# A four-layer recurrent kernel: the chunk inverse of layer 0 solved on 16x16 quarters, the last feed-forward's variances as columns, and a new written-out order

## The chip, the cores and the metric

The kernel runs on one core of a Trainium2 chip. The metric is device time in microseconds (us) of one execution; the times below are of three runs.

The core has five engines, each with an instruction queue of its own that it works off in order: PE (TensorE, matrix products; its weight loads are listed apart as PEld), DVE (VectorE), ACT (ScalarE), POOL (GpSimd) and SP (SyncE, which here only issues DMA transfers). They wait for one another by semaphores. Data lies in an on-chip memory of 128 partitions; PE writes into eight banks of 512 columns, from which DVE or ACT evicts the result. All data is 32-bit, and a matmul shows up in the profile as two instructions (two passes), a transpose as one.

## The reference, cut to what matters

Two sequences of 1024 tokens with 128 channels pass through four layers, each an attention and a feed-forward. Layer 0's attention is a delta rule in chunks of 32 tokens, 4 heads of 32:

```python
T = -einsum('bhnid,bhnjd->bhnij', k * beta, k)      # (k beta) k^T of a chunk, 32x32
T = where(tri_strict, T, 0.0)
for i in range(1, 32):                              # forward substitution
    T[..., i, :i] += einsum('bhnj,bhnji->bhni', T[..., i, :], T[..., :, :i])
T = T + eye(32)                                     # inverse of a unit lower triangle
u, w = T @ (v * beta), T @ (k * beta)
# then a scan over the 32 chunks: S = S + k_i^T (u_i - w_i S), o_i = q_i S + attn (u_i - w_i S)
```

The outputs of this rule, of two depthwise convolutions (7 and 25 taps) and of v itself are mixed by a small routed network. In layer 3 the feed-forward has two inner layers of local attention and a gated product behind a layer norm:

```python
mu, var = h.mean(-1), h.var(-1)
h = (h - mu) / sqrt(var + 1e-5) * lg + lb
a, g = split(h @ w1 + b1, 2)
x = x + (a * gelu(g)) @ w2 + b2
```

## The kernel before, in words

The kernel is first recorded and then issued. Every operation that `program` and the stage functions call goes to a recorder (`Record.note`), which bundles neighbouring small matmuls of one shape (up to 32) into one unit. Each unit knows which earlier units it depends on. A string, `ORDER`, is decoded into a list of all 7156 unit numbers, with a bit for each eviction that may run on DVE or ACT, which says which of the two takes it. `Record.issue` (its call is line 603, so that the profile names L603 for nearly every instruction) emits the units in that order. A second string, `PLACES`, says which physical buffer each tile gets. So each engine's queue is exactly the order's subsequence for that engine; no planner runs at build time. The two sequences (batches 0 and 1) are independent of one another, and the order interleaves them. The stage functions `l0_attn`, `l0_ffn`, `l1_attn` and so on are called per layer and per batch in `program`.

**Layer 0's attention** (`l0_attn`). After the projections and short convolutions, keys are transposed, normalized and kept in `ka`; `vk` holds, per token, v times beta and normalized k times beta (two DVE products per group out of the transposes' bank). Products of keys, 32x32 per chunk and head, land in the banks `kk`; DVE multiplies them by the mask `mb` (minus beta, strictly below the diagonal) into `nn`. Since the substitution works along rows, the 128 triangles (32 chunks x 4 heads) are brought one to a partition: eight transfers by way of the memory `scr_n` and one back into `ncol`. The substitution loop has 31 steps; step i multiplies i x i elements (`prod`) and sums them into column i of `u`. The result goes out to `scr_u` and returns in four transfers to `td`, tokens on partitions again. Then come `pu` (td times vk, 32x32 blocks at four row positions of the array, 64 matmul instructions a bank) and its eviction `uw`, then `chunk` and `au` products, the scan of 30 steps (`next` on PE, `state` on DVE), the outputs `o`, the convolutions on DVE (`conv`, 7 and 25 passes of 1024 columns), features, the small network (`rh`, `logit`), `mixed` and the output projection into `s`.

**Layer 3's feed-forward** (`l3_ffn`, `Block.forward`, eight times: two batches, two inner layers, two blocks of 512 tokens). Channels are on partitions. The product with the constant matrix `center` takes off the mean; ACT squares; the product with the constant `mean` (all 1/128) gives each token's variance in all 128 rows (`var`, 128x512); scale, root and reciprocal then run on 128x512, and `z` is multiplied by the result. `b2` is added by POOL after DVE has added the products `down`. `Block.forward` of the last block is followed by `close`, which gates and stores the output.

`t512` tiles have 512 columns and 21 buffers; `arr` tiles have 1024 columns out of 35 larger buffers; `small` tiles have up to 64 columns.

Of the kernel before, what the change touches and what calls it, by code (L numbers as in the profile page):

```python
# [21 lines left out]
ALU = mybir.AluOpType  # L22
X = mybir.AxisListType.X
# [165 lines left out]
def _constants():  # L189
# [12 lines left out]
        "ident32": (p % 32 == c[:, :32]) * one,  # L202
        "quad4": (p // 32 == c[:, :4]) * one,
# [52 lines left out]
def pack_inputs(inputs):  # L256
# [40 lines left out]
    "c-mE22VfM%*WWk0S90kgotn@U6j7x2-n&vokRnwO5J+;jdzS=|sv=zoC{22o9;rd3D_ufKLJ8?1$>r{L=X*1I@$Yv@Hd|(AUj4n_n|r?Wm%yTt"  # L297
    "sY21Fc7zfTd`khK>_P_+kM<M|<sMVm>#(Ad6JxR(+^PK!go{57stj4>hHB}it4-jh+WR+GzXvA=ysi7H`me;`>65j8IQ%>~I#awlz*T72?3s3?"
    "&6XLjMgJw^F7zt)gH@A76+-im-fGkjc8s#k2q~&L(Un{T2gE6Pl^@ok8M}K0LqMsYVVdk;dJjS(U%#UjI!*bZFX}u3$d1UaRUDcd`y@0_1m!u1"
    "pt-@n()eHI0Ni^A<%TOhTBAf8p4<q((K~Jd{P(kM=gTYn<Ro-HwRbh1bTm|PXI0A_@1Jg{PBXvY4_9xgUUkub-dZ{fb_~6F-BQ22>FUW)-vm`5"  # L300
    "rZPOJ427UQNrMsVCY*RWA?HfdqwdKs(_VSTA8)!#at*m8F6y}F6A@GpQ$qX0Pot?HIKe=T&e+Vi1`-QdhUE*{^e@nw1`_tD4ip5#^W=38w!1zz"
    "#z1nyyoE4v%|vVE1tZj$+2iWMgL+(?N3I5VoHVH+zdGCQ`iK0)|Luvc?0;GdlM60p4gra{JDxR>d=ZLAAIu2{zy00IjRk-90odD_5}_!l1G&37"
    "0Zs;3h^6L3r$9hlK5I+Ph@Yp6h9dY;$@PB$HB_*zoihIgtaPpLc@;4|cwU*gFt?USk|u@aYi^UJFp`>22Uc;GZkfJhW~Fn1(RHQ_u1BLD2RiK8"
    "_n}^t3NQvX!q^$j0=jJgNEuT&X*=cePXB(gQJk5ze4E$G(^rk{2*0oRue;_<4i31v!ZR(ZGQhK}mMy2XNQ0ul!LZ|I#x}@(e!qBvcVIfxUo254"
    "{bcNYk=>Y8cYJCGfHg4bsdNZn{JYZ|ynP0(F7A?>KK;F8jjZJ9emE-fHAHKmncz8IRCz(vy>W{dTn^jNpYHlJL?S<Y8ddsE2DnYV+D>nJt;#<G"
    "Z$sv@y)!FMiwp9(5aqkHU#+E~ty;pxR<O1D{;8R#<(#lrQRk=J#>uu1gQqc%mz8hGEF<e@Y|LD>ATGlY1<wmDwE#xPtMx#!qkA9KS#Wdbv~~j_"
    ">eX(5fv6n5TPY95!q*tfTSkKa8z29-;8y~elNM-l7Qly)F)x18Mr~buI>XPegaj5rWND4qokO+Xf}z>L@*$wzdkK(BE0Z-7Om4Fa=7IZr0tWCv"
    "Da`a5jG1{VsH-Ngn*KekoPy`<qe|g<TEHuRaelXkVhC}jd_rKpO-oFepSb?}8;SAr$4B~>5n@eFNW#DQkX0?i61r^W>?M!ZO=<FG_UD~$E!q6}"
    "qB-!(jflA;8bZjp@$1F;C4Mg|-)S&+YE^(4UsuamW|*A&VMaBWHMeZtxEfzUJ7`=>d*U|M*2K~*F-j`8h}zSbf1uWr*rMFp^l>An^I4b{Af-PH"
    "2`Oy+rbMfCB@7@6Ue?G7IM5Faxy2j5sH%PO^Rvn?X{$?w7!B$&J1z5Vd*oev>d#OzZhOhNpLTqqQiH(*`Mwrs>uV)Wvni;sq}suzvzK_(>LUj&"  # L310
    "JJPF$Y_yd5NiNZl3DN!;TEH|}^A9R2ClT3T3Mhb(Y_e;T=9Ef&;O7xrRrthUE(?22oghh)h{n|<greMc;nn}5mw5l(c_$j+lo?$c7ICMfQh_JH"
    "=_v}<0;na|Xz+Eq*28OXzl2}P&1JsjJ|#eWoE9Ia=3ij4l=x6LjedpU5g~Hyi&nwqgKH70nnX%9YN8?)f&5&(rGa=%nr8A4NhJga;0vk|-<=GT"
    "w$8tsmR>WwyZSY(FBU;GAAo)bdbw3%7Rx7eJ+Z39&rdaYRLMkCO%n}|>fi)Ui^rh3BN4yyAyhR`1Dyv8Aq&C^Je6JMS>GD7qE(ZoN`#2`4k14$"
    "%WE!Dl^B3{M2|^wH@OA@PU;~>_qwlsnBMsiR4SyF5`U-V%R>*%uG;BZ?W{7R5mcwYNA*E1e2N2|)I4Z!?X<8QKe8yfNVF7cVW7q*)w$^>k{hv="
    "syr|74=?I*7*x&F<HB1J1(e(-@R;19QDqikULbha<N+|cMcUx$`kv5Y+pMJKJ}oc3mBj9cZpf#)93q1jUKri;z{M`<FzsO9{UZGJo>&L=y_;9*"
    "`x!1UspR&D^kt-_MDi^)5O`MD|5WFD7I;g1FSj$E>3Fre)AG3BQE7+z&K)(*Z2Tgm(aS+^3Qr6<1U;%GLe;i0TdGG{J{sp*Z+f=*<%qK$ktH-8"
    "H=*6JkN*meJ@4ClRGWyPLP$=^UOngKj`d%XlW=^|v@c(taFQAsv}fn|&@5A8`8W3))T>%Ib`}j2bGrN;kY4Ma@zb=q6QqdC*7YI;zLhBITB%-U"
    ")r*5nAwR;DUD-oV=6<;rNFb2GDPLY{{wnm>mKS00=A_5JLa9lNd$#MND~1Inely0xrhYqfD!W(L+Og$C+v`xJTHK;;DStlvIy-EeM2Cvfp3=D6"
    "mvS@aLHdJUzn=Tf89>0^_}J>ZRp)d&tgihs97+&MELhjFEwf@pQfy(VMM}QdE*Vt~N&`ir($XMGd_<ZZ`PyjGeAHFjUOptXvkTVFh31#r<=m+U"
    "5w75kQRGeS{H%b$x7vwL2EQ(UuI~~<8oNwaKey+-zkcQ4SzGS@f^>vrRh2X);!DTqO~D0m!}r?kO5%5CZ{PI!t|;lro>fmvEKcc%>Ao{JjUMwZ"  # L320
    "nYpCQmS|Y;&c&4FLs-2ZlX9iQCs*$cztLpFXMs+Y_$qUJsasq<#$b9hpx=SCZ@~>Cs=xRNY`!46MG51uv{EsqYN^RdAgBm})dC-Lxw%~3^-UI~"
    "H5SfOT|jap&UGs!m+ICk6^$CK-FHA60Q>U~jDfz#x^JjLwdJ!h`9-(HBGf=sqMFep6eHEF8p}R*>$p(jM@fxm{PfbA?*btW)0m|lkVDYNRn{Ni"
    "^tV&}_w^v6L3|aelF_hPk~F$`?VshEIdA{i4dd(IS999I{nC%`1Qb-NdMy|{H8Vg}Yd@}a3xdjh0Qw(-H^BwrZ|*=7f2UD1Q(9&=AcR?pCC%T7"
    "08)+?aiXUPm0T9JEVPW2OMZ+4M*NIQV~P0j4`>RLS5-h-jHO)C4nPm_LH*J$BPaU5j)b(B8~t6SJ_~24XX{sfvHH+8DKDz#-?y69PNzhqNGd!>"
    "`ltWhn>^hq-@o;`sO#l%OMm$FOv<;FM|!kHMejZ98dwxuGy5Bpl2>=#f<NQipYD{=qDJK6*!OP_{`JD@3)MH)9s108AxgbGtXi$j)ok_J2OmDT"
    "{#DiefpxxF{7ur}l~c}s7u%PW%_5`#)|mF!q3fIMQs4Ub*F~!TRBwK{-jdc$JM?TB4brB#<wL%L@1tzdLknLW{W5>Y%yo6PE-NiCjQH(fPJpTF"
    "-23|?Hg!I>JZ^YF-r<0AiK|Dcucda0k18jA(cxD3?D$`1hW0tsq&_$bjFX>zHg0#p)s1Vmto-P!ix*oolx4q?Rb6~v&R*K;%Gr&bV%LxD(-%fH"
    "yC!%x7tGqQdgj^<^?tei24H2kVLw&b1s%KXm^9J7a|HFf(sb3e51v5G?MBx|{_0oavR58Y7u!~x*ewJXEG}E%dG}t+M&J7a%*)<YsaEw3{q{Gm"
    "aU=H6rXT-S5d2RO(p3sKu5}{$zmJ05P0sg8D}<)^>qB;6I`qjt7X4B{A`nhSl>X-QmAbxq9aZJ6>G$_Cu{svC-y7Ho_Vn2{=g6&30cvlQN(`!L"
    ")TYl|y9a;WqCBif?R4bUsudHq8>Xi8%Sc6%5s)6#(@0VVRL!hPOk~ZnM_Re>^OzO=4)|T$XHZ6N$z5?zEc<yXY#Ir%Gsl_<Eev`}mWEXCXWH3+"  # L330
    "|A)R%<DW~=IIv1VSv2Ikj<?-8E;uYFhd`Z2MV|BH5mNqc2t`4+8kt`O7wnz&B=*V5v4>$~nL8xtJM?Yy@D<gEO6vA;*6LFyCW1L-*!H12#+0f4"
    "?t5hs-!E_mmlAjIRK?Hfmk|QnnuMNqe?}z3`gU*LId^<%o-df3xsO9gB;3D0al@}e-}}=zXnW&Z9SguWJg6`aQm4LvK_^}uZx5+o6yR#sHRU3G"
    "llWp`Ro|B3Z|hjYr>%P9>sK_#4oJg#og44tgpg}D20qyn3waQKx|7n+e@C-UN}JF_eT%Qxd(iks{*28eE%`z7+t(q_(ktKO_iO7Wxn;Y^guH^t"
    "ACq4%^Z0iQh)w%2J@U}wm}jx1gC(UP?pc)os?XL37u5D-mxj?^N8fyPqV2w3dz;-)Z(+FKXWJ*o#%)iJB6-LJ@3!d|ym%ml<!p)>v#4a|5)kC2"
    "fy3u4*-%!Ov^A0w2KZ+poF34wb9o!6SEaDuXEo{!pPaKRetyeZ8B$PgGx0is_j2wBzD0a9w!LH+GHpdb%7ykLm*1>CVRqF<w?2GUquuqaH$J|l"
    "FRo4?7yho9J|3~~Tvq2QS8A6=yUr0~;FFpk!|AX~K@Zz}yt-w9TMM#Hf}EXw!7%0Iqp9m%0XDyZ5!(vC2hw`GpVV`yN37Gc+3nQ4E8m{EH&L@R"
    "D*onk!%w5J!+B>#|BZcCObXc9y^+=Dais^fCpCElAsPOwFRfql_0H7Lxmx4-@%K&NUE6H88n!)reDP+-;nO~7a^n;8@}UQvH#e4>S0oJa`=Bf<"
    "I&a?hpX_l4_dGgQ)WnQ~C#%BTBcI=@vOts|@==}g%c*&bMjZJvWeiM>dH$r=6ptA?{VuwfjSCp{tJVs>i(O}RLZ0YnYX7@f;v){)>^Ep*C=~jX"
    "6h)gpFMV{=HNdnZKlGFG+b@epUU`<@G3Z{u%Uf3NfyiIlL-$m*_b%vlss`k0?T@xjJGcbn<fId{&?3L`QHM#Bs|!Z_G;LX8`p`D#kF9J0^Y$#A"
    "J>bwv-`aBr)9Du%!kM%ge|$H?_1!Vi4u^yGbiOeB)$BGSrv3I^<14c-1xv1?w04W@4*Y(|f>j5OnJyJ|pVbMjo=Jqgw;GyP)&6r1EG}*Rr|H|H"  # L340
    "l=P_ELkgXXomAs%aIURzt^;YUw23B90?T4zQqK-C)lAjS?WuN*%D=Apy>D^-QFFpeo18uK#b3S1G4pBY5Jk7QFm|{ybcEx9aT7p7a#N#F-Bb5r"
    "-7~HTS6v87-P+$*^9lDn-dDN(@9m+@gNAMeTBP-CGQWl2tA23xy-Te?7NzE)2j!%Wr^-)m-bx&YO;Bd3-0j)rlN(Ze1H>$!YI!C#(C5`F4@6eV"
    "i+$m)iS;$BX3Nz95rx6zL7i)XMa^%MAphK8cu51R-VF#dzo1p}EP3fSy2sW!33uVi!#`HR2iUd5o;uoF8{%7fg?30WRi=-(kBfrGwKA$@m4n*$"
    "a&__ksHfTPC#?ah{W&+)T=u6cYY1$snl)U44P#HY+#!7$wTzB!HRhAuBT@$!!lvlgQBwQA#j4K|rnDZi^WMwM8m%9_ke-g!u0l~nd58V|bN$V`"
    "J6e8tzdiQUtu*z@zz6+~-EfNo5B1$UFS+)NeqYs#&f5K`>DAspu3q##oZHh3&J8cis*<&P27RT`D;+{ikB44-GjLhcjLI*DoqF@4@+Z5py5D)P"
    "HX-L<*S}LG<ki)fPdw)hEiONQ*Qd?{NfVzz2e;9a;Sw`DYR}wR)uiZ`o;v^3)U>l5mNe0>_gYj?X=8f&7W<6Fvz8}rJRP%Z-l@)mp}Y&+dA+^="
    "uxYJCi$}Y-sWVj5o(^oZv8>gfljFBOx~KI$d342;9*6U74QJ-heO~?PJL1(Q*Ud#|`$TqIDejrG{B%pxK=7Q*O6&wbPV2mN$oY@1or2kZ-^@>I"
    "|J$mQ2al8fXLFUSXXBhHUnI`lF?n11+gakG^j5i~&j-6AvK~(iJN9w#nqepYil}`xpry<C%>1DDAHFqB;>F-G8%%WP`<2Lhm%2X8Ibp8bX5D~+"
    "Pm8WlQZLk}`ut(nD=+zo^rhGK8<8Oy>UUpWf8b7^K5($_zMCHgz8M;{@kZmJz8eDC*I6^@U>B#96O;1M)4nNfZ)@Gl4Eub#8l8KG?CNtm@Y7}f"
    "6P5>&{LfFcK2Ahqv8DT|4rS&e{f@Ru?QTeU4?a4dKj3#uwm-Bz($xSbTp=w}ONRamJ)+hd%(O)){Pv;6QWCjgcz)Wz{oPbkQ0`IMtMK^eMURHT"  # L350
    "wjqz-TDE^tUh@7ui{=Bl<`_e|Gb1v5P0NmPGn~faIvFX7DoF{8#fR^TTe^m;rB45CpOyzrO}5IGfD5GV^D58k2i$518xPv*`e$c?5-)aZ`E%`z"
    "YR5k)k8$N;-*g$eQc25x`+m84lr)OTtWoyF)cshEGKu<#=DVHAiOBMgj#o3*mX20$7-xT6>q)Jnz5f>91@l|Ot;Pn=!<wa`(vd-h+dnaCf3?wG"
    "`~A^8Hxw*oK#ul2k9|?c3&Ya?X!XO4-x@qJQcrPMv$PebI`4p2LeuA=eoeoR3V!@<8-N{fXjDmVEh*)*vs!Dd#5XgvQt?}Zs}i!+Dp}{-5$w#%"
# [454 lines left out]
def cols(t, n=1, w=P):  # L808
    return slice(t * w, (t + n) * w)


def l0_attn(C, w, xpad, b, out):

    nc = C.nc
    H, DH, CH = 4, 32, 32
    NTH = TB * H

    fold = xpad.shape[1] > L
# [1515 lines left out]
```

## Time and profile before

| | |
|---|---|
| median of the three runs | 1892.36 us (1890.59 to 1892.56) |
| the profiled execution | 1896.98 us |
| its span, first to last instruction | 1895.1 us |
| PE busy | 1749.1 us (92%), 14012 instructions |
| DVE busy | 1399.5 us (74%), 2855 instructions |
| ACT busy | 1065.3 us (56%), 1980 instructions |
| POOL busy | 423.2 us (22%), 436 instructions |
| mean granted clock of PE | 0.948 of full |

Busy times are of the whole span, over stages that differ in what bounds them; that is why the prediction goes by stretches. PE's instructions are pipelined and their ends modelled, so that a busy PE need not be at its peak. A group's line has the line, engine, operation, tiles (written<-read), shape and count, then after the bar the busy time of the group in us, the mean of one in ns, and after the second bar the idle time of the engine just ahead of them with what ended most of it. A timeline's line has start and duration in us, and in brackets the idle time before and its releaser; "SPq" is the issue of a transfer. A stretch's line gives its two ends, its length, the busy time and count of each engine, PE's granted clock, the share of DMA time and GB/s.

### The profile page before, as it was taken

The page shows a single profiled execution, that of the slowest core. Times are in us where ns is not written, and L with a number is a line of the kernel's source. Part 1 is how long each engine was busy: PE and PEld are TensorE (multiplying, and loading weights), DVE is VectorE, ACT ScalarE, POOL GpSimd, SP SyncE. Part 2 cuts the span into 40 slices and gives each one's busy share as a digit, 9 for nine tenths or more (in the row PEclk, how much of TensorE's full clock was granted, in tenths as well). Part 3 has the DMA queues.
Part 4 walks back from the last instruction along what each step waited for, and adds up shares of the span by engine and source line. Part 5 has one row for each costly group of instructions (what it writes and reads, how often), then busy time and mean ns, then how long its engine had stood idle before and what let it go on. Part 6 is the DMA issues. An engine that isn't in the chain of part 4 may idle for free.

```text
span 1895.1 us, 35145 instructions
## 1 busy us (share of the span) xinstructions
PE 1749.1 (92%) x14012; PEld 995.0 (53%) x14012; DVE 1399.5 (74%) x2855; ACT 1065.3 (56%) x1980; POOL 423.2 (22%) x436
## 2 busy tenths in 40 slices
PE   7985996769999999999999999999999999999996
PEld 4454555554227632384665577544346776444483
DVE  7995999796115544345989897878889989877866
ACT  5231232226996588836646454765656777765552
POOL 0010102212221242303002640224307411620000
PEclk9995996679999999999999998999999999999998
DMA  3110101002223321332223022002002120001020
GB/s 111 30 23 9 23 23 35 13 1 59 85 79 103 111 62 39 92 103 72 67 61 100 26 89 68 1 2 58 12 14 64 39 60 29 1 2 38 10 85 21
DMA packets 67908, 90.91 MB, mean 48 GB/s; under 512 B 29185, under 2 KB 41473, under 8 KB 67617
## 3 DMA queue, kind: packets, MB, share of 16 engines
q1 hardware_dynamic: 58624, 59.34, 10.6%
q0 software_dynamic: 9120, 29.33, 5.4%
q8 instruction: 110, 1.80, 0.4%
q14 instruction: 54, 0.43, 0.1%
HBM read 80.65 MB, written 8.00 MB: 47 GB/s over the span
## 4 chain that ended last, share of the span: by engine, by line
PE 66%; DVE 24%; issue 4%; ACT 3%; DMA 2%; SPq 1%; POOL 0%; POOLq 0%; DVEq 0%; ACTq 0%
PE sim L603 16%; PE num L603 8%; PE av L603 7%; DVE u L603 4%; PE tr L603 4%; DVE conv L603 3%; PE wo L603 3%; PE down L603 2%; PE up L603 2%; DVE e L603 2%; DVE prod L603 2%; PE qk L603 2%; PE z L603 2%; PE ph L603 2%; DVE ss L603 1%
## 5 line engine op out<-in xcount | busy, mean ns | idle before, releaser
L603 ACT ACTIVATE e<-sim 128x512 f32<-128x512 f32 (+3 forms) x896 | 429.5, 558 | 166.3 <-PE sim L603 78.2
L603 PE MATMUL num<-e,v 128*64 128x512 f32 (+4 forms) x1280 | 188.5, 427 | 1.9 <-ACT e L603 1.2
L603 DVE TENSOR_TENSOR e<-e 128x512 f32<-128x512 f32 (+3 forms) x320 | 177.1, 588 | 9.5 <-PE num L603 4.0
L603 PE MATMUL sim<-q,kT 64*128 64x512 f32 (+3 forms) x768 | 158.5, 513 | 7.1 <-ACT e L603 4.5
L603 PE MATMUL sim<-q,k 32*128 32x512 f32 x1024 | 149.2, 641 | 0.0
L603 POOL TENSOR_TENSOR sq<-qk,tab 128x256 f32<-128x256 f32 x128 | 105.6, 851 | 140.6 <-ACT qk L603 62.7
L603 PE MATMUL av<-e,va 128*32 128x512 f32 x1024 | 135.4, 606 | 0.0
L603 PEld LDWEIGHTS num<-e,v 128*64 128x64 f32 x1280 | 80.7, 137 | 91.1 <-issue 69.4
L603 ACT ACT_TABLE_LOAD x89 | 114.2, 1283 | 16.2 <-DVE g L603 6.1
L603 PEld LDWEIGHTS sim<-q,kT 64*128 64x128 f32 x768 | 73.4, 186 | 94.8 <-ACT e L603 45.1
L603 PE MATMUL ph<-h,w_f 128*128 128x512 f32 x256 | 114.7, 601 | 0.8 <-ACT h L603 0.8
L603 DVE TENSOR_TENSOR sim<-sim,const 128x128 f32<-128x128 f32 x256 | 65.3, 291 | 42.4 <-PE sim L603 39.5
L603 PEld LDWEIGHTS sim<-q,k 32*128 32x128 f32 x1024 | 44.4, 184 | 99.3 <-ACT e L603 74.1
L603 POOL TENSOR_TENSOR u<-u,sq 128x512 f32<-128x512 f32 x64 | 88.2, 1393 | 5.4 <-issue 3.1
L603 ACT ACTIVATE e<-e 128x320 f32<-128x320 f32 (+3 forms) x160 | 77.7, 529 | 19.7 <-DVE e L603 18.8
L603 DVE SCALAR_TENSOR_TENSOR conv<-vT,w_a,conv 128x1024 f32<-128x1024 f32 x60 | 84.0, 1409 | 0.8
L603 PEld LDWEIGHTS ph<-h,w_f 128*128 128x128 f32 x256 | 48.1, 192 | 57.5 <-issue 55.2
L603 POOL DMA_INDIRECT we<-in_experts,index x46 | 44.7, 973 | 148.5 <-issue 29.4
L603 POOL DMA_INDIRECT xg<-xd,index x46 | 44.5, 967 | 148.5 <-DVE index L603 65.3
L603 DVE TENSOR_REDUCE ss<-sq 128x8 f32<-128x512 f32 x96 | 62.8, 672 | 8.2 <-ACT sq L603 8.2
L603 PE MATMUL qk<-w_f,shifted 128*128 128x512 f32 x128 | 62.5, 608 | 4.9 <-DVE shifted L603 2.2
L603 DVE SCALAR_TENSOR_TENSOR e<-sim,const 128x320 f32<-128x320 f32 (+2 forms) x128 | 62.3, 528 | 5.9 <-PE sim L603 4.3
(521 smaller groups left out, 3568.9 us busy)
## 6 DMA issues: line engine op xcount, KB each, us to landing
zb<-zd SPq DMA_DIRECT2D x192, 128.0 KB
tab<-in_rotary SPq DMA_DIRECT2D x8, 512.0 KB
yd<-y SPq DMA_DIRECT2D x10, 256.0 KB
w_f<-in_f SPq DMA_DIRECT2D x4, 512.0 KB
mk<-in_mask SPq DMA_DIRECT2D x4, 512.0 KB
w_l<-in_l SPq DMA_DIRECT2D x4, 512.0 KB
w_f<-in_f SPq DMA_DIRECT2D x4, 448.0 KB
w_f<-in_f SPq DMA_DIRECT2D x2, 516.0 KB
```

Of the source, the lines that this page charges most:

```text
L603: tc.keep_in_program_order(f(*map(real, args), **{k: real(v) for k, v in kw.items()}))
```

## The change

Three things are edited, and the order and buffer strings are replaced.

In layer 0 the two 16x16 triangles on the diagonal of each 32x32 triangle are inverted side by side: the loop has 15 steps, and step i works on 2 x i x i elements. The part left of the second triangle (16x16) is no longer solved; it is kept as `ko`, unscaled products of keys under the new mask `off32`. `td` holds both inverses on its diagonal, zeros elsewhere, and is multiplied by beta once; so `vk` holds v and k without beta. With D for `td` the chunk's solution is D (x - ko D x): one round of `pu` matmuls, an eviction, a second round with `ko`, a subtraction on DVE and a third round and eviction.

In the last feed-forward the variances are taken with the squares as weights, so that each group of 128 tokens gives one column (128x4 in all); scale, root and reciprocal run on these four columns; four products of the column, spread over 128 columns, with the identity matrix bring the result back to 128x512 in a bank. The eviction of the centred bank to `z` may go to ACT or DVE by the order's bit, where it was DVE's. The addition of `b2` on POOL stands ahead of the gated products.

The new order has 7176 units. In it batch 0's layer-0 attention ends at place 781 (before: 975), batch 1's at 1225 (before: 1148).

```diff
+        "off32": ((p % 32 < 16) & (c[:, :32] >= 16)) * one,
...
-    nc.vector.tensor_mul(rbeta, beta, rk)
...
-        nc.vector.tensor_tensor(vk[g][:, :, 1], heads(ps), bview(rbeta, 4 * g, 4), ALU.mult)
+        nc.scalar.copy(vk[g].rearrange("p (t h) s d -> p t h s d", h=H)[:, :, :, 1], ka[g][:, :, 0])
...
-        nc.vector.tensor_tensor(vk[g][:, :, 0], heads(ps), bview(beta, 4 * g, 4), ALU.mult)
+        C.evac(vk[g][:, :, 0], heads(ps))
...
                 nc.vector.tensor_tensor(
+                    four(ko, g, hp)[:, hh], pv[:, :, 0, :], C.c["off32"].unsqueeze(1).to_broadcast([P, 4, CH]), ALU.mult
+                )
...
         for q in range(4):
+            for a in range(2):
+                nc.sync.dma_start(
+                    out=scr_n[q, cols(g, 1, 16), a].rearrange("n i j -> i n j"),
+                    in_=nn[cols(2 * q + a, 1, HC), cols(g, 1, 16), cols(a, 1, HC)],
+                )
...
+    for i in range(1, HC):
+        pv = prod[:, : 2 * i * i].rearrange("p (a m j) -> p a m j", a=2, m=i)
+        nc.vector.tensor_tensor(
+            pv, u[:, :, 0:i, 0:i], n4[:, :, i, 0:i].unsqueeze(2).to_broadcast([P, 2, i, i]), ALU.mult
+        )
+        nc.vector.tensor_reduce(u[:, :, 0:i, i], pv, X, ALU.add)
+    nc.sync.dma_start(out=scr_u.rearrange("q n a j i -> (q n) (a j i)"), in_=ul)
+    ta = C.arr("td")
+    nc.gpsimd.memset(ta, 0.0)
...
+                out=td[cols(2 * q + a, 1, HC), :, cols(a, 1, HC)], in_=scr_u[q, :, a].rearrange("n j i -> j n i")
...
-    for i in range(1, CH):
-        pv = prod[:, : i * i].rearrange("p (m j) -> p m j", m=i)
-        nc.vector.tensor_tensor(pv, u[:, 0:i, 0:i], ncol[:, i, 0:i].unsqueeze(1).to_broadcast([P, i, i]), ALU.mult)
-        nc.vector.tensor_reduce(u[:, 0:i, i], pv, X, ALU.add)
...
+    nc.vector.tensor_tensor(td, td, bview(beta, 0, TB), ALU.mult)
...
-            C.evac(uw[g][:, 8 * k : 8 * k + 8], pu.rearrange("p (n s d) -> p n s d", s=2, d=32))
+            x, y = (v[g][:, 8 * k : 8 * k + 8] for v in (vk, uw))
+            C.evac(y, times(td, vk, g, k))
+            nc.vector.tensor_tensor(x, x, times(ko, uw, g, k), ALU.subtract)
+            C.evac(y, times(td, vk, g, k))
...
-            nc.vector.tensor_copy(z, pc)
-            pn = C.bank("var")
-            C.mm(pn, C.c["mean"], sq)
-            C.rstd(r, pn, 1.0, 1e-5)
-            nc.vector.tensor_mul(z, z, r)
+            pn, pr = C.bank("vcol"), C.bank("roots")
+            for k in range(4):
+                C.mm(pn[:, k : k + 1], sq[:, cols(k)], C.c["mean"][:, :1])
+            C.rstd(r, pn[:, :4], 1.0, 1e-5)
+            for k in range(4):
+                C.mm(pr[:, cols(k)], r[:, k : k + 1].to_broadcast([P, P]), C.ident)
+            C.evac(z, pc)
+            nc.vector.tensor_mul(z, z, pr)
             nc.vector.tensor_scalar(z, z, w["lg"], w["lb"], ALU.mult, ALU.add)
+            nc.gpsimd.tensor_tensor(tiles(xb), tiles(xb), w["b2"].unsqueeze(1).to_broadcast([P, 4, P]), ALU.add)
...
             nc.vector.tensor_add(xb, xb, ps)
-            nc.gpsimd.tensor_tensor(tiles(xb), tiles(xb), w["b2"].unsqueeze(1).to_broadcast([P, 4, P]), ALU.add)
```

`times` holds the matmul loop of `pu` as it stood before, with the matrix as an argument.

## The prediction on record

> **What bounds the kernel now.** I read the page's 40 slices first, then the busy time by stretch, then groups inside the first 420 us, then two timelines.
>
> ```profile
> PE   7985996769999999999999999999999999999996
> DVE  7995999796115544345989897878889989877866
> PEclk9995996679999999999999998999999999999998
> ```
>
> A slice is 47.4 us. In the first nine VectorE (DVE) is fullest, TensorE (PE) has holes and its granted clock dips to 0.6; after that PE is at nine tenths almost throughout. The stretches say it in us:
>
> ```profile
> core 0: us, PE busy (x) PEld busy (x) DVE busy (x) ACT busy (x) POOL busy (x), PEclk, DMA share, GB/s
> 0.00:420.00 420.00, 333.92 (x4530) 208.16 (x4530) 358.37 (x639) 128.28 (x191) 55.24 (x52) 0.83 0.11 30
> ...
> 420.00:1000.00 580.00, 572.46 (x3913) 290.33 (x3914) 292.01 (x790) 398.67 (x728) 130.53 (x142) 0.98 0.26 76
> 1000.00:1840.00 840.00, 806.21 (x5345) 470.51 (x5345) 713.94 (x1382) 522.80 (x1041) 234.47 (x240) 0.99 0.13 39
> ```
>
> Layer 0 of both batches ends at 415 us (last write of `s`, batch 1: 415.5). Up to 420 us DVE works 358 and idles 62, of which 10 at the start and some 25 in batch 0's recurrence (`next`/`state`, 144 to 182 us). So layer 0 is DVE's. From 420 us to 1840 us PE idles 42 us in 1420: DVE savings there can win only from those. The last 55 us are one chain.
>
> **Part 1, substitution (layer 0).**
>
> ```profile
> L603 DVE TENSOR_TENSOR prod<-u,ncol 128x1 f32<-128x1 f32 (+30 forms) x62 | 34.6, 558 | 1.7
> L603 DVE TENSOR_REDUCE u<-prod 128x1 f32<-128x1 f32 (+30 forms) x62 | 31.2, 504 | 1.9
> L603 PE MATMUL pu<-vk,td 32*32 32x64 f32 x512 | 11.8, 257 | 5.3 <-issue 4.6 <-DMA td<-scr_u 0.7
> ...
> L603 DVE TENSOR_TENSOR mixed<-mixed,rms 128x1024 f32<-128x1024 f32 x4 | 4.9, 1219 | 0.0
> ...
> L603 DVE TENSOR_TENSOR nn<-kk,mb 128x128 f32<-128x128 f32 x16 | 3.9, 281 | 0.7 <-PE kk L603 0.6
> ```
>
> Step i of the old loop works on i² elements, i = 1 to 31. The tile's rows give 0.140 us at one element and 1.16 at 961, so 0.139 us + 1.063 ns an element. The new loop has i = 1 to 15 on 2i²: 30 instructions of 0.139 (4.2 us) and 2 x 2480 elements (5.3 us), 9.4 us a batch. Old 34.6 + 31.2 = 65.8 us for both batches, new 18.9: **47 us less**. Added on DVE, both batches: 16 `ko` products at 0.281 (4.5), two scalings of `td` at 1.22 (2.4), eight subtractions of 512 columns at 0.68 (the DVE rows of that size; 5.4). The `vk` writes: eight of 0.68 (5.4) go from DVE, all but one of them to ACT; two more `uw` evictions land on DVE (1.4). Net -38 us. The order's bits also move other evictions of layer 0 to DVE (16 to 23 of 52, +5.6 us): layer 0 sums to 326 us of DVE work before and 293 after, **-33**.
>
> PE gets 16 more groups of 64 small instructions: at 11.8 us for eight now (1.5 each), 24 us; at the densest stretch (192 in 2.88 us), 15. PE idles 86 us up to 420, so beside DVE this costs nothing; if PE became the bound, 15 to 24. ACT gains 13 copies of 512 columns (0.58 each, 7.5 us) and idles 292 us there.
>
> DMA: `scr_n` goes from 8 to 16 transfers a batch and `td` from 4 to 8, with rows of 64 bytes in place of 128, as many rows in all. The trace has no such row. The trip now:
>
> ```profile
> 281.71 0.32 SPq L603 DMA_DIRECT2D scr_u<-u  x1
> 284.37 4.21 SPq L603 DMA_DIRECT2D td<-scr_u  x4
> ...
> 290.25 0.19 PEld L603 LDWEIGHTS pu<-vk,td 32*32 32x32 f32 x6 [0.63 <-DMA td<-scr_u]
> ```
>
> 8.5 us from issue to the first use. With half the bytes, bounds are -4 (time goes with bytes) and +9 (with transfers); I take 0, since the number of rows is unchanged. Its cover: between `scr_u` and the first user of `td` the new order has 8 us of DVE work in batch 0 and 12 in batch 1. Queued behind it are the three dependent rounds of `pu` (matmul, eviction, matmul, subtraction, matmul, eviction): two more rounds of about 1 + 0.7 + 0.3 us, 4 to 6 us of chain, over which the order puts 9 us of DVE work in batch 0. SP issues 24 more transfers at 0.3 to 0.6; it waits for DVE and ACT most of the time, so nothing. The memsets of `td` are POOL's (0.95 us for 1024 columns), with 365 us free.
>
> **Part 2, the order.** I decoded both ORDER strings and summed trace durations. In front of batch 1's last layer-0 work stand 369 us of DVE work before (358 as busy time, since ends overlap) and 353 after. So of the 33 us, half shortens layer 0 and the other half is filled with later layers' work (45 us of it before, 60 after). PE work of later layers ahead of that point grows too, from 37 to 81 groups of matmuls of layer 1; sized by columns at 0.43 us for 512 (eight `ph` passes take 3.44) that is about 10 us. Batch 0's attention now ends with 242 us of DVE work ahead of it, not 319. With DVE idle as long as now, layer 0 ends 16 us earlier (400), and PE then has 10 us less before it: **-25 us** (16 + 10, rounded down because DVE sums overlap). The order of layers 1 to 3 is close to the old one: positions of each stage's end move by under 110 of some 7160.
>
> Idle time could grow. The recurrence of batch 0 took 32 us (151.6 to 183.6) over 18 us of DVE work; the new order has 24 us over it, better. That of batch 1 took 36 us over 32; now 23, so up to 10 us of cover go.
>
> The Trainium skill, "TensorE: Matmul & The Clock Gate", section "What's actually happening", says that an idle window of about 3.4 us halves PE's clock; a wait inside the three-round chain would then be paid twice. The granted clock was 0.66 in 300 to 400 us and 1.00 in 500 to 600; read by the rule, the array was at half speed for two thirds of the first stretch. By the rule one such window for each batch would add some 3 us, an estimate, and the sum would be 1863; by the rows it is the one below.
>
> **Part 3, last feed-forward, eight times.** Removed from DVE: a reciprocal of 512 columns and a scale of 0.68; put in: the same on four columns.
>
> ```profile
> L603 DVE RECIPROCAL r<-r 128x512 f32<-128x512 f32 x8 | 26.8, 3345 | 1.2 <-ACT r L603 1.0
> ...
> L603 PE MATMUL var<-sq,const 128*128 128x512 f32 x16 | 8.6, 617 | 2.1 <-ACT sq L603 2.1
> ...
> L603 DVE TENSOR_SCALAR r<-var 128x512 f32<-128x512 f32 x8 | 5.4, 681 | 1.8 <-PE var L603 1.7
> ```
>
> The four-column reciprocals of this trace take 0.12 and small scales 0.15, so 8 x (3.35 + 0.68 - 0.27) = 30 us; six of eight `z` copies go to ACT (4 us). PE loses two passes of 0.43 and gains eight 1-column instructions (nearest row `ss`, 32 in 3.63 us: 0.91) and eight of 128 columns (tr, 8 in 0.87: 0.9 to 1.0): +1 us each.
> The path: PE is busy under seven of the eight reciprocals (3.3 of 3.35 us); the chain of waits runs through that at 1606 us and the first of the last two (1865). So in the six before the tail, DVE's 28 us give something only where PE idles (34 us in 1000 to 1840): bounds 0 and -25, taken -9, a third. PE's extra: +6. In the tail the chain `var` 1.14, scale 0.70, root 0.64, reciprocal 3.37 becomes 0.9 + 0.15 + 0.2 + 0.12 + 1.0: -3.5.
>
> ```profile
> 1887.02 1.64 POOL L603 TENSOR_TENSOR xn<-xn,w_f 128x512 f32<-128x512 f32 x1 [1.41 <-DVE xn L603]
> 1888.70 0.63 ACT L603 ACTIVATE sg<-xn 128x512 f32<-128x512 f32 x1 [2.42 <-POOL xn L603]
> ```
>
> The POOL addition of `b2` stood in the last chain (1.64) and now comes earlier, beside the matmuls: -1.6. Against it, the new order moves the last layer norm of the attention (four DVE passes of 1.2) into that tail, between the chain's steps: +1. Tail **-4**.
>
> **Sum**: -25 + 6 - 9 - 4 = -32 us. The profiled execution took 1896.98 (span 1895.1 and 1.9 around it) and would take 1865; it lies 4.6 above the median of the runs, 1892.36, so **1860 us**.
>
> **Rivals.**
> *All of it comes through* (0.20). DVE's idle time in layer 0 shrinks, because the 33 us and the better cover both count: -33 - 10 there, -20 in layer 3, -4 in the tail: 1825. For it: layer 0 has no engine fuller than DVE. Against: chains, not DVE, end the waits in the recurrence.
> *Cover is lost* (0.16). Two DMA trips at +9 and 10 us of the second recurrence uncovered, some already filled: +20, so 1880.
> *PE's clock becomes layer 0's bound* (0.09, the slower case). PE is busy 334 us at a mean clock of 0.83 up to 420. If batch 0 runs alone through three-round chains and PE starves, the clock falls as it does in 300 to 400 us (0.66). Some 277 us of full-speed work (334 x 0.83) plus 20 new, at 0.66: 450 us, 35 past 415; less 10 of PE work done ahead and 7 in layer 3 and the tail: +18, so 1910. It decides from a clock of about 0.69 (297/0.69 = 430).
> *Nothing* (0.05): order and PE's additions eat it, 1892.
>
> Forecast 0.50, its own spread 1845 to 1875. Range: 1822 to 1886 takes in most of the forecast, half of the first rival and most of the second, about 0.8. Within 0.2% (3.8 us, about what a measurement of this kernel can tell from no change) holds 0.05, plus 0.01 of the second rival; slower 0.10 with a stray; faster 0.84.
>
> **What would show it.** Right: `prod` and `u` near 19 us busy together, DVE's busy time down 60 to 70 us in all, layer 0's last `s` near 400 us, no reciprocal of 512 columns, PE still full from 400 on. Wrong: the last `s` after 415; PE's clock under 0.70 up to 400 us; more than 80 us of DVE idle before it; PE's idle time after 420 us above today's 42.

## The result, and the profile after

The changed kernel takes **1863.87 us** (median of 4 runs, 1863.17 to 1867.5) against 1891.47 for the kernel before (4 runs): ratio 0.9863, 95% interval 0.984 to 0.9886. The profiled execution took 1864.44 us, with a span of 1862.7.

The 40 slices after (46.6 us each), and the busy time by stretch:

```profile
PE   7985899679999999999999999999999999899987
DVE  6775988686213643246889898889987978978865
PEclk9895899588999999999999999999999999999989
```

```profile
0.00:420.00 420.00, 341.90 (x5540) 212.01 (x5541) 319.26 (x603) 133.45 (x196) 50.86 (x52) 0.86 0.09 24
420.00:1000.00 580.00, 572.96 (x3964) 294.23 (x3964) 302.30 (x793) 412.25 (x740) 138.07 (x149) 0.99 0.26 80
1000.00:1840.00 840.00, 809.63 (x5570) 493.48 (x5569) 701.04 (x1404) 516.74 (x1040) 227.35 (x239) 0.99 0.12 38
```

The columns are those shown before. Up to 420 us VectorE (DVE) lost 39 us of work (358.4 to 319.3), and idles 39 us more (62 to 101): the relief turned into waiting. Batch 1's last `s` begins at 437.1, not at 416.3 as before (the prediction's 415.5 is the end of the first of batch 1's two writes of `s`). The forecast named both as signs that it was wrong, and yet its time is right.

So where did the time go? A common measure is needed, since the two orders do different work at the same time. I added up the cost of the matmuls that all kernels share (without `pu`, `var`, `vcol`, `roots`) in the order in which they ended, and compared the times at which the same sum was reached. Each matmul counts with the mean time from its start to the next one's start, over all of its kind in the traces before and after, long gaps cut off. The first row of the table gives time in the kernel before, the others how much later (+) or earlier (-) a kernel gets that far, in us. The other kernels are explained below.

| same PE work as before at | 218 | 368 | 468 | 813 | 992 | 1158 | 1287 | 1409 | 1642 | 1810 | end |
|---|---|---|---|---|---|---|---|---|---|---|---|
| changed kernel | +15 | +18 | +4 | 0 | -4 | -3 | -23 | -31 | -25 | -31 | -31 |
| substitution alone | +18 | +31 | +29 | +27 | +27 | +28 | +27 | +27 | +30 | +29 | +28 |
| columns alone | -3 | -1 | -2 | -4 | -4 | -4 | -2 | -2 | +3 | +3 | +7 |
| both edits, old order | +28 | +40 | +38 | +37 | +37 | +40 | +41 | +41 | +47 | +47 | +51 |
| new order, old code | +57 | +82 | +68 | +65 | +62 | +63 | +55 | +48 | +77 | +71 | +76 |
| new order, columns | +59 | +85 | +71 | +68 | +65 | +65 | +45 | +38 | +45 | +39 | +38 |
| new order, substitution | +16 | +20 | +4 | +3 | -1 | 0 | -8 | -16 | +13 | +8 | +13 |
| new order and columns in layer 3 alone | -3 | -1 | -3 | -4 | -4 | +26 | +24 | +23 | +30 | +34 | +33 |
| new order and substitution in layers 0 to 2 alone | +15 | +23 | +8 | +6 | +3 | +44 | +54 | +55 | +59 | +65 | +64 |
| kernel before, `pu` three times | +12 | +22 | +20 | +19 | +18 | +19 | +18 | +18 | +19 | +19 | +18 |
| changed kernel, added groups merged | +8 | +10 | -4 | -7 | -10 | -10 | -30 | -38 | -33 | -39 | -40 |

How the matmuls are weighed matters where the new order stands in other work than the old: with columns in place of times, its rows move by up to 16 us at 218 and 13 at 1158, but by 4 at most at 813, 992 and from 1409 on.

**The changed kernel gains next to nothing until 992 us.** By 1409 it is 31 us ahead, so it gains 27 in the stretch in which batch 0 begins layer 3, and at the end it is 31 ahead still. In the kernel before, one gap stands at the start of that stretch (its trace, as a row of the timeline and as a stretch; then the same stretch after):

```profile
1164.71 2.08 PE L603 MATMUL q<-w_a,xlT 128*128 128x512 f32 x2 [3.71 <-DVE u L603]
```

```profile
1158.00:1200.00 42.00, 37.95 (x207) 28.90 (x204) 30.71 (x51) 21.46 (x44) 1.71 (x1) 0.84 0.13 39
```

```profile
1158.00:1200.00 42.00, 41.84 (x383) 32.86 (x380) 36.11 (x69) 32.14 (x55) 2.56 (x3) 1.00 0.17 53
```

PE waited 3.71 us for DVE's `u`, and its granted clock was 0.84 in those 42 us; after, PE is full at 1.00. The Trainium skill, "TensorE: Matmul & The Clock Gate", section "What's actually happening", says that an idle window of about 3.4 us sends the clock to half. This trace agrees in kind, since the granted clock was 0.50 from 1162.5 to 1176.2 us; but it fell when PE had been idle for some 1.5 us, since 1161.0.

**In layer 0** the chain from the loop to the end of `pu` shows what was given back. By the first and last rows of the tiles (start of the first, end of the last, in us):

| | first `prod` | last `u` | first `pu` | last `pu` |
|---|---|---|---|---|
| batch 0 before | 78.0 | 123.8 | 137.5 | 147.8 |
| batch 0 after | 89.4 | 101.6 | 114.6 | 148.0 |
| batch 1 before | 231.9 | 281.6 | 290.2 | 302.5 |
| batch 1 after | 273.4 | 290.3 | 301.0 | 334.9 |

The loop of each batch is 33 us shorter (45.8 to 12.2; 49.7 to 16.9), but `pu` lasts 33 us in place of 10 and 12: of 33 us won in each batch, 22 to 23 went back. The loops also begin later, by 11 and 41 us; how much of that is the new order's choice and how much is waiting was not separated. The rows of PE inside it (changed kernel, timeline, with the rows between left out) show how:

```profile
118.55 0.42 PE L605 MATMUL pu<-vk,td 32*32 32x64 f32 x16 [1.30 <-issue]
...
123.75 0.58 PE L605 MATMUL pu<-uw,ko 32*32 32x64 f32 x26 [1.74 <-issue]
...
127.47 0.58 PE L605 MATMUL pu<-uw,ko 32*32 32x64 f32 x26 [1.74 <-issue]
...
138.66 0.77 PE L605 MATMUL chunk<-ka,uw 32*32 32x64 f32 x56 [1.72 <-issue]
...
142.11 0.73 PE L605 MATMUL chunk<-uw,ka 32*32 32x32 f32 x56 [2.07 <-issue]
...
146.12 1.81 PE L605 MATMUL pu<-vk,td 32*32 32x64 f32 x58 [2.22 <-issue]
```

PE stops for 1.3 to 2.2 us with nothing to wait for that the profile shows. Counted in the trace, exactly 128, 128, 384 (three times 128), 128 and 128 matmuls lie between these stops, and where all of them are small the stops come every 3.45 to 4.0 us. A small matmul in a dense run thus costs 27 to 31 ns, not the 15 that 192 in 2.88 us had suggested. What DVE waits for in layer 0, after and then before (waits up to 420 us: total, times, longest):

```profile
DVE state L605 <- PE next L605: 28.4, 42, 3.2
DVE nn L605 <- PE kk L605: 11.0, 4, 5.6
DVE uw L605 <- PE pu L605: 9.3, 3, 4.2
DVE step L605 <- PE chunk L605: 5.7, 1, 5.7
DVE vk L605 <- PE pu L605: 5.5, 3, 3.0
```

```profile
DVE state L603 <- PE next L603: 19.7, 37, 1.7
```

All five are waits for small matmuls. The kernel before had 2.8 us at `step`, 0.6 at `nn` and none at `uw` and `vk`, but 6.4 at `add`, which waits for `chunk` too. Of the 39 us more of idle time, 14.8 are waits for `pu` itself.

### The profile page after: what moved, and what is told of

It is laid out like the page before. It is cut to its first block, busy times and chain, and to the rows that moved or that the text cites. A ratio compares the mean times of both kernels' runs of the same rounds, so it can differ in the third digit from the quotient of the medians.

```text
span 1862.7 us, 37413 instructions
## 1 busy us (share of the span) xinstructions
PE 1739.7 (93%) x15148; PEld 1009.8 (54%) x15148; DVE 1335.7 (72%) x2819; ACT 1070.6 (57%) x1988; POOL 416.3 (22%) x440
## 4 chain that ended last, share of the span: by engine, by line
PE 79%; DVE 10%; issue 4%; ACT 3%; DMA 1%; POOL 1%; SPq 1%; DVEq 0%; POOLq 0%; ACTq 0%
PE sim L605 16%; PE num L605 8%; PE ph L605 6%; PE av L605 6%; PE wo L605 5%; PE tr L605 4%; PE down L605 3%; PE qk L605 2%; PE up L605 2%; PE z L605 2%; DVE u L605 2%; PE p L605 2%; PE nd L605 1%; PE q L605 1%; PE pu L605 1%
## 5 line engine op out<-in xcount | busy, mean ns | idle before, releaser
L605 PE MATMUL num<-e,v 128*64 128x192 f32 (+4 forms) x1280 | 183.7, 426 | 2.2 <-ACT e L605 2.2
L605 DVE TENSOR_TENSOR e<-e 128x512 f32<-128x512 f32 (+3 forms) x320 | 171.6, 574 | 16.4 <-PE num L605 9.1
L605 PE MATMUL sim<-q,kT 64*128 64x512 f32 (+3 forms) x768 | 147.7, 504 | 1.5 <-ACT e L605 1.5
L605 POOL TENSOR_TENSOR sq<-qk,tab 128x256 f32<-128x256 f32 x128 | 98.6, 797 | 219.9 <-DVE ss L605 98.5
L605 PE MATMUL ph<-h,w_f 128*128 128x512 f32 x256 | 119.3, 622 | 0.0
L605 DVE SCALAR_TENSOR_TENSOR conv<-vT,w_a,conv 128x1024 f32<-128x1024 f32 x60 | 78.3, 1312 | 0.9
L605 PEld LDWEIGHTS av<-e,va 128*32 128x32 f32 x1024 | 21.5, 108 | 85.1 <-issue 75.7
```

The source lines that it names most:

```text
L605: tc.keep_in_program_order(f(*map(real, args), **{k: real(v) for k, v in kw.items()}))
```

## The experiments

The change has three separable parts: the substitution, the columns, the order. ORDER and PLACES name units by number, so an order for other code was projected: units that both codes share keep their order, new ones stand where their inputs and the unit that follows them put them, and buffers are assigned again where a place was taken. Such a run holds a cost of misplaced units as well as the effect of the edit. The last four runs change no unit and no order, and carry the verdicts on sizes.

### Each part without the others

**Both edits in the order before** (`edits_old_order`): ORDER and PLACES of before, projected on the changed code.

> Both edits (substitution on quarters, variances as columns), with the order of before: shared work keeps its place, new work stands right behind what it depends on. Theory (the 28 us come from layer 3's DVE relief, where PE's gaps and its lowered clock between 1160 and 1410 us go; layer 0's 33 us of DVE are given back as waits): 1865 to 1875 us. Rival A (the new order of layer 3 does it): 1883 to 1890. Rival B (the substitution does it, by an earlier start of layer 1): 1865 to 1875 too, with layer 0 ending before 400 us.

Measured: 1940.08 us, ratio 1.0243 [1.0226, 1.026].

**The old code in the new order** (`old_code_new_order`): the code of before, with the changed ORDER projected.

> The code of before with the order of after (shared work in its new place). Theory: no gain, 1890 to 1920 us, since the order was laid out for less DVE work. Rival A (the order does it): 1865 to 1875.

Measured: 1972.47 us, 1.0419 [1.0401, 1.0436].

**The columns alone** (`ff_alone`), in the order before:

```diff
...
-            C.mm(pn, C.c["mean"], sq)
-            C.rstd(r, pn, 1.0, 1e-5)
-            nc.vector.tensor_mul(z, z, r)
...
+            for k in range(4):
+                C.mm(pn[:, k : k + 1], sq[:, cols(k)], C.c["mean"][:, :1])
+            C.rstd(r, pn[:, :4], 1.0, 1e-5)
+            for k in range(4):
+                C.mm(pr[:, cols(k)], r[:, k : k + 1].to_broadcast([P, P]), C.ident)
+            C.evac(z, pc)
+            nc.vector.tensor_mul(z, z, pr)
...
```

> Only the variances as columns and the earlier b2 addition, with the order of before. Theory: most of the gain, 1868 to 1876 us (4 to 5 of it in the tail), and PE's granted clock from 1160 to 1200 us at 0.95 or more where it was 0.83. Rival A: the tail alone, 1886 to 1888. Rival B: the same as rival A.

Measured: 1901.52 us, 1.0043 [1.0026, 1.006].

**The substitution alone** (`sub_alone`), in the order before, with layer 0's part of the diff:

> Only the substitution on quarters, with the order of before. Theory: little, 1885 to 1893 us; DVE's busy time up to 420 us falls by some 30 and its idle time grows by as much. Rival B: 1865 to 1872, layer 0 ending 25 us or more earlier than 415.

Measured: 1926.44 us, 1.0172 [1.0143, 1.0202].

All four missed: no part is faster by itself, and both edits together are slower than either. The theory of that time, that the columns are the gain, falls, and so do both rivals as gains that stand alone. By the table of leads, the substitution has lost all of its 28 us by 368 us, in layer 0.

### Which half of the order, which edit inside it

**Layer 3 new, the rest old** (`l3_new_only`): the code of before with the columns; layers 0 to 2 in the old order, layer 3 in the new.

> Layers 0 to 2 as before the change (old substitution, old order), layer 3 with the columns and in the order of the changed kernel. By the lead in equal PE work the changed kernel is level with the old one until 1158 us and gains 25 us from there to 1409 and 6 in the tail. Theory (layer 3's code and order together make the gain, layer 0 gives nothing): 1860 to 1870. Rival A (the gain in layer 3 stands on how far the two batches are apart when they enter it, which layers 0 to 2 of the new order set): 1885 to 1905. Rival B (layer 0's 39 us of DVE work is the gain): 1885 to 1900.

Measured: 1925.11 us, 1.0156 [1.0124, 1.0188].

**Layers 0 to 2 new, layer 3 old** (`l02_new_only`):

> The other half: the new substitution and the new order in layers 0 to 2, layer 3 with the old code in the old order. Theory (layer 3 alone gives the gain): 1885 to 1897, level with before. Rival A (the distance of the batches): 1865 to 1880, if the old order of layer 3 lets it come through. Rival B (layer 0): 1860 to 1870.

Measured: 1954.74 us, 1.0322 [1.0296, 1.0348].

Both miss every figure. The leads say where: each is close to the kernel before until 992 us (-4 and +3) and loses 30 and 41 us from there to 1158 us, at the joint, where batch 0 enters layer 3 while batch 1 is still in layer 2. Two halves of different orders don't fit there. What these two runs settle is only that layer 3's order brings nothing when the work of the other batch around it stands in the old order.

**The new order without the columns** (`no_ff`):

> The changed kernel's order throughout, with its substitution, but the last feed-forward's variance as full 512-column tiles again. Gives the worth of the columns inside the new order. Theory (DVE's 28 us in the forwards and PE's order there are one gain): 1885 to 1897. Rival C (the gain of layer 3 is that of its order, the columns bring no more than the tail's 4 us): 1865 to 1870.

Measured: 1909.64 us, 1.0086 [1.0062, 1.0111]: 46 us over the changed kernel (42 by the two ratios to the kernel before), more than either expected. It lies level with the changed kernel until 992 us (-1 and -4) and falls 35 us further behind it by 1642 us (+13 and -25). PE's waits for the normalized `z` (total, times, longest), in this kernel, in the changed one and in the kernel before:

```profile
PE g L591 <- DVE z L591: 11.6, 4, 4.7
```

```profile
PE g L605 <- DVE z L605: 0.3, 1, 0.3
```

```profile
PE g L603 <- DVE z L603: 1.6, 1, 1.6
```

In the new order PE waits for the forwards' DVE chain. These rows show 11.6 of the 46 us; what share the misplaced units have, this run can't tell.

**The new order without the substitution** (`no_sub`):

> The changed kernel's order throughout, with the columns, but the old one-quarter-after-the-other loop of 31 steps in layer 0. Gives the worth of the new substitution inside the new order. Theory (layer 0 gives nothing net, but the new order counts on 39 us less of DVE work): 1880 to 1900, the new order made slower in layer 0 by up to those 39 us. Rival A (layer 0's time is hidden, only layer 3 counts): 1862 to 1870. The run of the old code in the new order lost 80 us before 430 us, so a figure near 1940 is possible: then the order of layer 0 is worth nothing without the substitution, and the two stand together.

Measured: 1930.12 us, 1.0186 [1.0153, 1.0219]. It is 85 us behind at 368 us, and then gains 27 from 992 us to the end, as the changed kernel does (27). So layer 0's time is not hidden, as rival A had it, but is paid in full, and the gain of layer 3 is the same whether layer 0 is late or not: the expectation's last case, that the new order's layer 0 is worth nothing without the substitution.

The eight corners together (us; the kernel before was 1893 beside these runs and 1891 beside the changed kernel):

| | neither edit | substitution | columns | both |
|---|---|---|---|---|
| order before | 1893 | 1926 | 1902 | 1940 |
| new order | 1972 | 1910 | 1930 | 1864 |

Each edit costs in the old order (+33 and +9) and gains in the new (-62 and -42, each without the other). All but 1893 and 1864 are of projected orders and so hold a cost of misplaced units.

### Sizes, with no unit and no order changed

**`pu` three times** (`pu_thrice`), kernel before:

```diff
-            for op, args, kw in u.ops:
+            for op, args, kw in u.ops * (3 if first.startswith("pu.") else 1):
```

> The kernel before, with every matmul of `pu` issued three times in place (the same operands and target): PE gets the 1024 small matmuls that the change adds, and nothing else changes, no order and no dependency. In the changed kernel, dense runs of 32x32 matmuls stop for 1.2 to 2.2 us after each 128, so that 128 take 3.45 to 4.0 us. Theory (the stream of PE's instructions sets the price of the added rounds): 8 x 3.5 to 4 = 28 to 32 us on PE, most of it in layer 0's chain: 1910 to 1925. Rival (my prediction: 15 to 24 us of PE beside DVE, at no cost): 1890 to 1897.

Measured: 1918.71 us, 1.0134 [1.0117, 1.0151], so +24 us by the medians, 25 by the ratio, and 18 between the two profiled executions. The theory's range holds; the prediction's "costs nothing" falls. Groups of PE (busy, mean ns, idle before), first this kernel, then the changed one:

```profile
L609 PE MATMUL pu<-vk,td 32*32 32x64 f32 x1536 | 30.4, 243 | 11.6 <-issue 11.6
```

```profile
L605 PE MATMUL pu<-vk,td 32*32 32x64 f32 x1024 | 20.2, 230 | 5.5 <-issue 5.5
L605 PE MATMUL pu<-uw,ko 32*32 32x64 f32 x512 | 9.4, 215 | 3.9 <-issue 3.9
```

Busy plus stops: 42.0 here, 11.8 + 4.6 = 16.4 before, so +25.6, and the time grew by most or all of that. By the table of leads it was lost by 368 us, in layer 0, and never came back: PE's rounds stand in layer 0's chain. The changed kernel has 39.0, +22.6. Batch 1's last `s` moved from 416.3 to 438.8.

**The added groups as one matmul each** (`pu_merged`), changed kernel; the result of the rounds is another:

```diff
+            ops = u.ops
+            if u.n in whole:
+                (ps,), kw = u.ops[0][1:]
...
+                ops = [("matmul", (flat(ps, BLK),), dict(
+                    lhsT=flat(kw["lhsT"], P), rhs=flat(kw["rhs"], BLK), start=True, stop=True))]
-            for op, args, kw in u.ops:
+            for op, args, kw in ops:
```

> The changed kernel, with the 32 small matmuls of each added group (second and third round) issued as one matmul of 128x128 by 512 columns on the same tiles, which computes something else: the evictions, subtractions, waits and the order stay. PE loses 1024 records and gains 32 of 0.43 us. Theory (the stream): 28 to 32 us go, 14 come, so layer 0 ends 10 to 20 us earlier, 1844 to 1856. Rival (the waits of the dependent rounds and the order in PE's queue make the loss, not the number of instructions): 1860 to 1868.

Measured: 1854.73 us (1853.29 to 1857.2), 0.9789 [0.9773, 0.9805]: 9 us under the changed kernel (14 by the two ratios to the kernel before), at the slow end of the theory's range and outside the rival's.

```profile
L613 PE MATMUL pu<-vk,td 128*128 128x512 f32 x16 | 10.2, 736 | 0.0
L613 PE MATMUL pu<-vk,td 32*32 32x64 f32 x512 | 8.6, 215 | 2.3 <-issue 2.3
L613 PE MATMUL pu<-uw,ko 128*128 128x512 f32 x16 | 8.4, 619 | 0.0
```

Busy plus stops are now 29.5 in place of 39.0, 9.5 less, and the last `s` begins at 429.4, 7.7 earlier. The large matmuls took 0.58 us, not 0.43, which is why less came than 10 to 20. By the table of leads 8 us of the 9 are there by 468 us and stay. Again the time followed PE's busy time and stops, about one for one.

**The reciprocals as copies** (`r_copy`), kernel before; the normalization is left out of the value:

```diff
+            if u.stage == "l3_ffn" and ops[0][0] == "reciprocal" and ops[0][1][0].shape[-1] == BLK:
+                ops = [("tensor_copy", a, k) for _, a, k in ops]
```

> The kernel before, with the eight reciprocals of 512 columns replaced by copies in place (0.68 us for 3.35), which computes something else: 21 us less on VectorE, in the old order, with no other unit changed. Theory (in the old order PE is full under the reciprocals, so only the tail's 2.7 us and a little come): 1883 to 1891. Rival (the relief is worth 20 us in itself, and the run with the columns alone lost it by the place of the `roots` matmuls): 1868 to 1880.

Measured: 1895.62 us, 1.0003 [0.9992, 1.0014].

```profile
L606 DVE COPY r<-r 128x512 f32<-128x512 f32 x8 | 3.4, 420 | 1.8 <-ACT r L606 1.7
```

26.8 us of reciprocals became 3.4, and nothing came of 23 us: even the tail's 2.9 don't show in the interval. In the tail two rows say why, first that of before, then that of this run: behind the next-to-last block's `z`, DVE's queue has the scale of the last block's variance, which waits for PE's `var`. The time that the reciprocal gave up became that wait. (`var` took 1.85 us there, at a granted clock of 0.50, and 1.13 before, at 1.00.)

```profile
1869.09 0.68 DVE L603 TENSOR_SCALAR r<-var 128x512 f32<-128x512 f32 x1
```

```profile
1870.06 0.69 DVE L606 TENSOR_SCALAR r<-var 128x512 f32<-128x512 f32 x1 [3.17 <-PE var L606]
```

In the old order that DVE work is covered. So the +9 us of the columns alone come from their `vcol` and `roots` matmuls or from misplaced units, which no run tells apart. (The expectation's 21 us took 0.68 for a copy; it takes 0.42.)

**The column reciprocals 29 times** (`r_long`), changed kernel:

```diff
+            if u.stage == "l3_ffn" and ops[0][0] == "reciprocal" and ops[0][1][0].shape[-1] == 4:
+                ops = ops * 29
```

> The changed kernel, with each of the eight four-column reciprocals of the last feed-forward issued 29 times in place (an odd number, so that the value is the same): 28 x 0.12 = 3.4 us more on VectorE in each forward, 27 in all, as the old reciprocal had; order and units stay. Theory (in the new order the forwards' VectorE chain is uncovered, as the run with the wide variance in the new order says, 46 us over the changed kernel): 1880 to 1895. Rival (that loss came from the places of the other units): 1864 to 1872.

Measured: 1922.35 us, 1.0148 [1.0127, 1.0169], 58 over the changed kernel (54 by the two ratios), beyond the theory's range of 16 to 31. The group, the first of the eight chains in the timeline, and who waited for `root` (total and times, rows between left out):

```profile
L608 DVE RECIPROCAL root<-root 128x4 f32<-128x4 f32 x232 | 41.3, 178 | 9.8 <-ACT root L608 2.1
```

```profile
1162.91 6.12 DVE L608 RECIPROCAL root<-root 128x4 f32<-128x4 f32 x29
```

```profile
who waited for it (us, times):
...
  PE roots L608: 33.2, 7
```

The dose was mis-sized: 29 in place took 6.12 us, 0.21 from one start to the next, where the expectation had 0.12 (the shortest of four in the trace before). So 5.9 us were added to each forward, 48 in all, and not 27. All of it came through in the new order, and 6 to 10 us more, for which no run shows the reason. The rival (1864 to 1872), that the wide variance in the new order lost only by misplaced units, falls.

## Why the prediction was right in its number and wrong in its main step

**The number**: 1860 forecast, 1863.87 measured; the profiled execution 1864.44 against 1865. The -32 us of the sum came as -32.5 between the profiled executions, from other places: layer 0 was to bring -25 and brought next to nothing, layer 3 with the tail was to bring -7 and brought about -28. That the two misses cancel is luck.

**DVE's relief in layer 0**: sized well. `prod` and `u` took 19.7 us (18.9 said), DVE's busy time to 420 us fell by 39 (33 said).

**The failed step** is the cover: "PE idles 86 us up to 420, so beside DVE this costs nothing; if PE became the bound, 15 to 24", with "DVE idle as long as now". The runs put in its place: busy plus stops of `pu` grew by 22.6 us, so the price of 15 to 24 was right and "nothing" was not; the same 1024 matmuls added to the kernel before, nothing else changed, cost 24 us, and taking 9.5 us of them out of the changed kernel gave 9 to 14. PE's free time was not free, since it lies in the waits of the same chain: while PE works through a round, DVE waits for it. An engine that is fullest in a stretch need not bound it. The prediction's own row of `pu` shows 4.6 us of stops beside the 11.8 us that it priced. Layer 0 was to bring -25 and the lead is 0 at 813 us, -4 at 992.

**The DMA trip**, taken as 0 between -4 and +9: from the last `u` to the first `pu` 13.0 and 10.7 us. The trace before gave 8.5 us from issue to use in batch 1, so +2 there; inside the bounds. In batch 0 the first `pu` stood as late in the old order (13.7).

**The forwards**: -9 + 6 predicted, -27 came from 992 to 1810, more than the bound of -25 that took all of the relief. The reason given for a third, that PE was busy under seven of the eight reciprocals, is right for the old order: relief alone brings 0 there. What failed is "the order of layers 1 to 3 is close to the old one: positions of each stage's end move by under 110 of some 7160". A small move of each stage's end says nothing of how the units lie inside: 23 us less of DVE work are worth nothing in the old order (`r_copy`), and 48 us more cost 54 to 58 in the new (`r_long`).

**The tail**: -4 predicted. From the end of the last `center` to the last instruction the kernel before took 28.3 us and the changed one 24.9, so -3.4; with the columns alone, in the old order, it took 31.2. The last layer norm of the attention (rows of `ln_sq`, `ln_v`, `s`) lies beside the forward's matmuls, and the last addition feeds `sg` directly, with no POOL row between (changed kernel, timeline):

```profile
1836.92 1.22 DVE L605 TENSOR_TENSOR s<-s,ln_m 128x1024 f32<-128x1024 f32 x1
...
1855.30 0.69 DVE L605 TENSOR_TENSOR xn<-xn,down 128x512 f32<-128x512 f32 x1 [1.99 <-PE down L605]
...
1856.07 0.63 ACT L605 ACTIVATE sg<-xn 128x512 f32<-128x512 f32 x1 [2.10 <-DVE xn L605]
```

**The rivals**: none was the case as a whole. *Cover is lost* was right about layer 0, by another mechanism (PE's rounds; the DMA trip lost 2 us, and the second recurrence, which was to lose 10, went from 36.4 to 34.2 us), and its loss was hidden in the total by layer 3. *PE's clock* didn't decide: 0.86 up to 420 us, 0.83 before.

**Open**: which moves inside the new order make layer 3's 27 us. Transplanting layer 3's order alone didn't bring it, but the joint lost 30 us there, so that run can't tell whether the gain needs the batches as far apart as the new order has them: every run with the gain has the new order in all layers. The new order without the columns gets some 15 us from 992 to 1409 us (-1 to -16) and loses 29 after it, so part of the gain there is order and part columns; a single move wasn't isolated. How much of the loss of the substitution in the old order (33 us) is PE's rounds (24 by `pu_thrice`) and how much places that an order made for it would better, can only be said as that sum.

## What to carry to other kernels

Before work on the fullest engine is traded for small instructions on an engine with holes, look whether the holes lie in the same dependent chain; there they are no cover, and each added instruction is paid in full. Price a dense run of small matmuls by its mean over several hundred, stops included, and test it by issuing it again in place. An edit and the hand-written order that carries it are one thing: judge a saving by what is late next in the order that it will run in, since 23 us less on VectorE were worth nothing in one order, and 48 us more cost 54 to 58 in the other.

## What the runs showed of the hardware that was not expected

PE stops at every 128th matmul of a dense run of 32x32 tiles, or at a multiple of it, for 0.8 to 2.4 us. Stops over 0.8 us with no releaser number ten up to 450 us in the kernel before (15.8 us) and sixteen after (26.1 us); none comes later, where the matmuls are longer. In a dense run the count between two of them is 128 or a multiple of it, a record or two missing. With the 128 weight loads these are 256 instructions. The Trainium skill, "Runtime: NRT & Kernel Launch", section "Instruction fetch mechanics", says that an engine's instructions are refilled in blocks of 256 and that crossing a block is mostly hidden.

The traces show that refill. One DMA queue of the kind "instruction" moves packets of 16384 bytes, as many as PE's instructions have blocks of 256, rounded up (28024 instructions and 110 packets before, 30296 and 119 after; packets, MB, share of the DMA time):

```profile
q8 instruction: 110, 1.80, 0.4%
```

```profile
q8 instruction: 119, 1.95, 0.4%
```

In both traces every one of the 26 stops ends 1.28 to 1.62 us after a packet of this queue has landed. In a dense run these packets start 3.3 to 5 us apart; from 450 us on they are at least 7.3 us apart, and there "mostly hidden" agrees with the trace. In layer 0's dense runs it does not. Where between the two the limit lies, no run tried.

Of DVE, 29 four-column reciprocals in place, each on the result of the one before, took 6.12 us: 0.21 us from one start to the next, 0.178 of it the instruction.
